# Attention behind a scan: fetching keys a group earlier, dividing the last query pair in SBUF, summing experts in one PSUM bank

## The chip, the cores and the metric

The kernel runs on one core of a Trainium2 chip. A core has a matmul engine (TensorE; PE in the profile, with PEld for its weight loads), a vector engine (DVE), a scalar engine (ACT), GpSimd (POOL) and a sync engine (SP) that here issues nearly all DMAs. Each engine runs its own instructions in order and waits for others by semaphores. SBUF is the working memory, PSUM the memory that TensorE writes. The metric is device time in microseconds (us); lower is better.

## The reference

Input `x` is 4 images of 128 channels and 64 x 64 pixels. Layer 0 is a group norm, a convolution block and a state-space scan (4 groups of channels, 16 states each), added to `x`. Layer 1 takes the 4096 pixels of an image as tokens and does attention with 4 heads and a mixture of 8 experts, of which each token uses 2:

```python
qkv = (x @ W_qkv + b_qkv).reshape(b, n, H, D, 3)
...
scores = jnp.einsum('bhnd,bhmd->bhnm', q, k) * scale
att = jax.nn.softmax(scores, axis=-1)
out = jnp.einsum('bhnm,bhmd->bhnd', att, v)
...
router_probs = jax.nn.softmax(x @ router_w + router_b, axis=-1)
top_p, top_i = jax.lax.top_k(router_probs, K)
...
return jnp.einsum('bnk,bnkc->bnc', top_p, gathered)
```

All is float32.

## The kernel before, in words

**Slots.** Image `b` has 4096 tokens, cut into 8 blocks of 512 (`BLK`, `NB`). One loop of slots (from L1381) runs everything. The scan has 512 units, of two slots each, so `END = 2 * len(units)` is slot 1024; slots behind that have no scan. In a slot the kernel writes out, in a fixed order: sends that have come due (`flush`), the fetch of a scan row (`rows`), a half step of lane X, one group of attention scores, their exponentials, the scan's DVE work, half steps of lane Y, the transposed sums of the scan (`y`), then the value products of the group before (`weighted`) and a second half step of lane X. `queued` (L389) fixes this order on each engine, SP included: what is written first is issued first.

**Attention.** Query blocks go in pairs `q` (1024 queries), key blocks in runs (`RUNS`, L904), since keys become known only as the scan proceeds. A run is cut into parts of one or two key blocks (n = 1 or 2) for each of 4 heads; there are 80 parts an image, 320 in all. A part is worked off in groups of two key tiles (`STEP`, L872), one group a slot: two groups for n = 1, four for n = 2. `load` (L948) fetches a part's queries (`qs`, two buffers; only where head or query pair is new), keys (`ks`, three) and values (`v`, three). L973 decides when the next part is loaded. Where it isn't there when a part begins (keys not yet computed), the part loads for itself and waits two slots.

**The end of a head.** In `weighted` (L1000) the sums of a head and query pair are copied or added from PSUM into `avs`: for each of the two query blocks u, 32 rows of products and 32 rows with the softmax denominator. If more keys are to come, `avs` goes to DRAM as `avd`, to come back as `prev`. Otherwise it goes to DRAM as `total`. When all 4 heads of a pair are there, `inverted` (L1031) loads the denominators packed as `den`, inverts them, stores them as `inverse`, and appends two output tasks, one for each query block.

**Outputs.** `finished` (L1051) is an output task on lane X, or on lane Y behind the scan. It loads `aT` (products), `inv` (inverse denominators, repeated over rows) and `acc` (the residual), multiplies, projects with `wp` into PSUM, adds, normalises, routes, and then applies the experts in four pairs: `share` (a pair's weights, repeated over all partitions by a 512 KB load) times `xf` on DVE, two matmuls with `ew` into the lane's PSUM bank, one DVE add into `res`. Each lane has one PSUM bank.

The last image's last pair (q = 3) runs its keys in one run, (3, 0, 8), behind the scan.

Of the kernel before, what the change touches and what calls it, by code (L numbers as in the profile page):

```python
# [9 lines left out]
F32 = mybir.dt.float32  # L10
# [7 lines left out]
P = 128  # L18
C = 128
EPS = 1e-5  # L20
BLK = 512
NT = BLK // P
# [3 lines left out]
DH = 32  # L26
NH = 4
NE = 8
# [8 lines left out]
def conv_mamba_attn_moe_kernel(ctx: ExitStack, tc: tile.TileContext, t: dict):  # L37
    nc = tc.nc
    x, out = t["x"], t["out"]
    B, _, L = x.shape  # L40
    NB = L // BLK
# [11 lines left out]
    def load(name, shape=None, src=None, eng=nc.sync, pool=const):  # L53
        src = t[name] if src is None else src
        w = pool.tile(list(shape or src.shape), F32, name=f"w_{name}")
        eng.dma_start(out=w, in_=src)
        return w
# [25 lines left out]
    wv, wp, rw, ew, eb8 = (load(k, eng=late) for k in ("wv", "wp", "rw", "ew", "eb8"))  # L83
# [13 lines left out]
    for j in range(4):  # L97
        r = slice(DI * (j % 2), DI * (j % 2) + DI)
# [301 lines left out]
    class Queue:  # L400
# [7 lines left out]
    tensor, vector, scalar, gpsimd, sync = (  # L408
        Queue(e) for e in (nc.tensor, nc.vector, nc.scalar, nc.gpsimd, nc.sync)
    )  # L410

    def mm(out, lhsT, rhs, start=True, stop=True):
        tensor.matmul(out, lhsT=lhsT, rhs=rhs, start=start, stop=stop)
# [8 lines left out]
    def send(out, in_, slots=1):  # L422
        outgoing.append([slots, out, in_])
# [14 lines left out]
    def pool(name, bufs=1, space=None):  # L438
        return main.enter_context(
            tc.tile_pool(name=name, bufs=bufs, **({} if space is None else {"space": space}))  # L440
        )

    att, mix, side = pool("att"), pool("mix"), pool("side")
# [4 lines left out]
    def work(lane, shape=None):  # L448
        return ps_work.tile(shape or [P, BLK], F32, tag=f"work{lane}", name=f"ps_{lane}")

    def tmp(lane, name, shape=None):
        return side.tile(
            shape or [P, BLK], F32, tag=f"tmp{lane}", name=name, bufs=6 if lane == "X" else 4
        )
# [417 lines left out]
    STEP = 2  # L872
# [57 lines left out]
    def attention(b):  # L930

        seen, parts = {}, []
        for q, lo, hi in RUNS:
            known = seen.get(q, 0)
            seen[q] = known + hi - lo
            cuts = [lo, *range(lo + 2 - lo % 2, hi, 2), hi]
            for h in range(NH):  # L940
                for k0, k1 in zip(cuts, cuts[1:]):
                    parts.append((
                        q, h, k0 // 2, k0 % 2, k1 - k0, k0 == lo, k1 == hi, known > 0,
                        seen[q] == NB,
                    ))
        assert all(n == NB for n in seen.values())

        def load(part, qs=None):  # L948
            q, h, k, u, n = part[:5]
            if qs is None:  # L950
                qs = queries(b, q, h)
            return qs, keys(b, h, k, u, n), values(b, h, k, u, n)

        prev = None
        ahead = None
        for at, part in enumerate(parts):
            q, h, k, _, n, first, last, more, final = part
            position[0] = b, parts, at
            if ahead is None:
                while not ready(b, part):  # L960
                    yield None
                ahead = load(part)
                for _ in range(2):
                    yield None
            qs, ks, v = ahead
            ahead = None
            for g in range(0, NT * n, STEP):
                if g == 0 and last:
                    prev = None
                    if more:  # L970
                        prev = att.tile([P, BLK], F32, name="prev", bufs=2)
                        sync.dma_start(out=prev, in_=partial.pop((b, q, h)))
                if g >= NT * n - 3 * STEP and ahead is None and at + 1 < len(parts):  # L973
                    nxt = parts[at + 1]
                    if ready(b, nxt):
                        ahead = load(nxt, qs if nxt[:2] == (q, h) and not nxt[5] else None)
                scs = []
                for j in range(g, g + STEP):
                    sc = ps_sc.tile([P, 2, BLK], F32, name="sc")
                    for u in range(2):  # L980
                        mm(
                            sc[:, u, :], ks[:, j * P : (j + 1) * P],
                            qs[:, u * BLK : (u + 1) * BLK],
                        )
                    scs.append((v[:, j // NT, j % NT, :], sc))
                yield (
                    b, q, h, scs, first and g == 0, last and g + STEP == NT * n, prev, final,
                )

    sums, partial, total, inverse, later = [None], {}, {}, {}, deque()  # L990
# [9 lines left out]
    def weighted(group):  # L1000
        b, q, h, pTs, first, last, prev, final = group
        if first:
            sums[0] = ps_av.tile([P, BLK], F32, name="av")
        av = sums[0]
        for k, (v, pT) in enumerate(pTs):
            for u in range(2):
                mm(
                    av[64 * u : 64 * u + 2 * DH, :], v, pT[:, u, :],
                    first and k == 0, last and k == STEP - 1,
                )  # L1010
        if last:
            avs = att.tile([P, BLK], F32, name="avs", bufs=2)
            if prev is None:
                scalar.copy(avs, av)
            else:
                vector.tensor_add(avs, av, prev)


            if not final:
                partial[b, q, h] = dram.tile([P, BLK], F32, name=f"avd{q}{h}")  # L1020
                send(partial[b, q, h], avs, 3)
                return
            if h == 0:
                total[b, q] = dram.tile([2, 2, NH, DH, BLK], F32, name=f"total{q}")
            d = total[b, q]
            send(d[:, :, h].rearrange("u k r q -> (u k) r q"), avs, 3)
            if h == NH - 1:
                work_left = inverted(b, q)
                later.extend((slot + n, work_left) for n in (4, 6, 8))

    def inverted(b, q):  # L1031

# [15 lines left out]
            ))  # L1048
        yield

    def finished(b, qb, lane):  # L1051

        q, u = divmod(qb, 2)
        td = kqv[b][3]
        s = slice(qb * BLK, (qb + 1) * BLK)
        acc = side.tile([P, NT, C], F32, name="acc", bufs=2)
        aT, inv = tmp(lane, "aT"), tmp(lane, "inv")
        sync.dma_start(out=aT, in_=total[b, q][u, 0].rearrange("h d q -> (h d) q"))
        sync.dma_start(
            out=inv, in_=inverse[b, q][u][:, None, :].to_broadcast([NH, DH, BLK])  # L1060
        )
        sync.dma_start(out=acc.rearrange("p j c -> p (j c)"), in_=td[:, s])
        yield
        yield
        yield
        vector.tensor_mul(aT, aT, inv)
        yield
        ps = work(lane, [P, NT, C])
        for j in range(NT):
            mm(ps[:, j, :], aT[:, j * P : (j + 1) * P], wp)  # L1070
# [4 lines left out]
        ps = transposed(lane, acc)  # L1075
        yield
        xf = tmp(lane, "xf")
        scalar.copy(xf, ps)
        yield
        ps = work(lane, [P, NT, NE])  # L1080
# [45 lines left out]
        ps = work(lane)  # L1126
# [3 lines left out]
        prT = tmp(lane, "prT")[0 : 2 * NE, :]  # L1130
# [16 lines left out]


        ps = work(lane)
        mm(ps, eb8, prT[0:NE, :])  # L1150
        yield
        res = tmp(lane, "res")
        vector.tensor_add(res, ps, xf)
        yield
        ahead = deque(share(e) for e in (0, 2))
        yield
        yield
        for e in range(0, NE, 2):
            if e + 4 < NE:
                ahead.append(share(e + 4))  # L1160
            yield
            w = ahead.popleft()
            if e:
                vector.tensor_add(res, res, ps)
            vector.tensor_mul(w, w, xf[:, None, :].to_broadcast([P, 2, BLK]))
            yield
            ps = work(lane)
            for u in range(2):
                mm(ps, ew[:, e + u, :], w[:, u, :], u == 0, u == 1)
        yield  # L1170
        vector.tensor_add(res, res, ps)
        send(out[b][:, s], res, 2)
        yield

# [94 lines left out]
    lanes, done, running = {"X": deque(), "Y": deque()}, set(), {}  # L1269
# [50 lines left out]
    X, Y = lanes["X"], lanes["Y"]  # L1320
# [9 lines left out]
    for k in range(-2, len(blocks)):  # L1330
        if 0 <= k:
            b, i = blocks[k]
            Y.append((("in", b, i, 1), inputs(b, i, 1), [("scan", *blocks[k - 1], 1)] if k else []))
        if k + 2 < len(blocks):
            b, i = blocks[k + 2]
            if k + 2 == 0 or i > 0:
                upper(k + 2)
        if 0 <= k + 1 < len(blocks):
            b, i = blocks[k + 1]
# [19 lines left out]
    END = 2 * len(units)  # L1359

    rows, due, closing, y_of = {}, deque(), deque(), {}
    h_of, slot = {}, 0
# [18 lines left out]
    while (  # L1381
        slot < END or due or closing or summing or waiting or left or later or lanes["X"] or running
    ):
        at, odd = divmod(slot, 2)
# [10 lines left out]
        if unit and not odd:  # L1395
            h = h_of.pop(at)
# [31 lines left out]
        if waiting:  # L1428
            weighted(waiting)
# [11 lines left out]
    with tc.If(nc.values_load(general[0:1, 0:1]) > 0):  # L1441
# [4 lines left out]
        with tc.For_i(0, B, 1) as b:  # L1446
# [3 lines left out]
                out=t_tok.rearrange("p k c -> p (k c)"),  # L1450
                in_=tsave[bass.ds(b, 1)].rearrange("o p q -> (o p) q"),
            )
            with tc.tile_pool(name="ps_again", bufs=4, space=PSUM) as psum:
                for i in range(NB):
                    ps = anew(t_tok[:, NT * i : NT * (i + 1), :], psum)
# [92 lines left out]
```

## Time and profile before

| what | us |
|---|---|
| median of 3 runs (5158.14 to 5181.4) | 5163.62 |
| the profiled execution's own time | 5160.79 |
| its span, first to last instruction | 5158.6 |
| last DVE instruction of the scan starts at | 4578.8 |
| last attention product ends at | 5087.5 |

The profile is of one execution. It gives each engine's busy time and instruction count, groups of instructions with mean duration and the idle time of the engine before them, and a chain of work followed back from the last instruction. Nearly all instructions were recorded through one helper, so their line reads L406 and they are told apart by the tiles they write and read: `sc<-qs,ks` are scores, `av<-pT,v` value products. A weight load or matmul of 512 columns can stand as two or more records.

| shares of the chain that ended last | |
|---|---|
| PE | 58% |
| DVE | 17% |
| ACT | 11% |
| DMA | 7% |

DMA issues of the tiles that the change touches:

| tile | issues | KB each |
|---|---|---|
| `ks` | 192 and 128 | 512 and 256 |
| `v` | 192 and 128 | 256 and 128 |
| `qs` | 161 | 512 |
| `rows` (the scan's) | 1024 | 512 |
| `share` | 128 | 512 |

### The profile page before, as it was taken

The page shows a single profiled execution, that of the slowest core. Times are in us where ns is not written, and L with a number is a line of the kernel's source. Part 1 is how long each engine was busy: PE and PEld are TensorE (multiplying, and loading weights), DVE is VectorE, ACT ScalarE, POOL GpSimd, SP SyncE. Part 2 cuts the span into 40 slices and gives each one's busy share as a digit, 9 for nine tenths or more (in the row PEclk, how much of TensorE's full clock was granted, in tenths as well). Part 3 has the DMA queues.
Part 4 walks back from the last instruction along what each step waited for, and adds up shares of the span by engine and source line. Part 5 has one row for each costly group of instructions (what it writes and reads, how often), then busy time and mean ns, then how long its engine had stood idle before and what let it go on. Part 6 is the DMA issues. An engine that isn't in the chain of part 4 may idle for free.

```text
span 5158.6 us, 62573 instructions
## 1 busy us (share of the span) xinstructions
PE 4703.0 (91%) x20684; PEld 2317.3 (45%) x20684; DVE 3835.7 (74%) x5780; ACT 3743.0 (73%) x5700; POOL 433.5 (8%) x483
## 2 busy tenths in 40 slices
PE   4567898999999999999999999999999999999997
PEld 2333444444444444444444444444444444443443
DVE  6988767877778878877788787877888887752422
ACT  4556777887787777787878787787788787765453
POOL 1111111110000110010000100010000001000000
PEclk7778999999999999999999999999999999999997
DMA  4556567677666667676766767667866667764532
GB/s 127 182 189 214 206 212 253 234 235 244 232 226 226 232 230 255 230 241 234 265 236 207 235 218 273 239 227 245 286 219 221 221 234 258 239 212 163 177 130 68
DMA packets 451692, 1131.70 MB, mean 219 GB/s; under 512 B 51857, under 2 KB 135330, under 8 KB 451362
## 3 DMA queue, kind: packets, MB, share of 16 engines
q1 hardware_dynamic: 447296, 1125.96, 64.5%
q8 instruction: 166, 2.72, 0.2%
q10 hardware_dynamic: 4066, 1.67, 0.1%
q14 instruction: 164, 1.34, 0.1%
HBM read 967.22 MB, written 143.39 MB: 215 GB/s over the span
## 4 chain that ended last, share of the span: by engine, by line
PE 58%; DVE 17%; ACT 11%; DMA 7%; issue 4%; POOL 2%; SPq 1%; DVEq 0%; ACTq 0%; POOLq 0%
PE av L406 25%; PE sc L406 14%; PE ps_X L406 9%; PE ps_Y L406 6%; PE y L406 6%; DVE h L406 6%; ACT pT L406 4%; ACT L406 3%; DMA ks<-kd 2%; DVE hc L406 2%; DMA rows<-bcd 1%; ACT xt L406 1%; POOL rsX L406 1%; DMA inv<-inverse 1%; DVE stX L406 1%
## 5 line engine op out<-in xcount | busy, mean ns | idle before, releaser
L406 ACT ACTIVATE pT<-sc 128x1024 f32<-128x1024 f32 x2048 | 1984.9, 1023 | 923.4 <-PE sc L406 922.3
L406 PE MATMUL av<-pT,v 128*64 128x512 f32 x8192 | 2003.1, 610 | 6.4 <-DVE avs L406 6.3
L406 PE MATMUL sc<-qs,ks 128*128 128x512 f32 x4096 | 1298.7, 436 | 91.3 <-DMA ks<-kd 47.8
L406 DVE TENSOR_TENSOR_SCAN h<-da,state,h 128x1025 f32<-128x1025 f32 x512 | 1204.2, 2352 | 91.8 <-ACT h L406 58.2
L406 PEld LDWEIGHTS sc<-qs,ks 128*128 128x128 f32 x4096 | 701.1, 190 | 820.2 <-ACT pT L406 272.7
L406 PEld LDWEIGHTS av<-pT,v 128*64 128x64 f32 x8192 | 500.5, 137 | 838.6 <-issue 813.5
L406 ACT ACTIVATE da<-delta,amat 128x512 f32<-128x512 f32 x1024 | 744.4, 731 | 1.9
L406 PE MATMUL y<-ident,hc 128*128 128x128 f32 x4096 | 622.3, 283 | 58.4 <-DVE hc L406 58.4
L406 DVE TENSOR_TENSOR hc<-rows,h 128x1024 f32<-128x1024 f32 x512 | 624.4, 1220 | 15.7 <-PE y L406 5.4
L406 DVE TENSOR_TENSOR h<-rows,du 128x1024 f32<-128x1024 f32 x512 | 623.4, 1218 | 13.0 <-DMA rows<-bcd 13.0
L406 PEld LDWEIGHTS y<-ident,hc 128*128 128x128 f32 x4096 | 520.8, 147 | 219.0 <-issue 76.0
L406 POOL TENSOR_TENSOR rsX<-rsX,mhalf 128x4 f32<-128x4 f32 x92 | 203.7, 2214 | 2668.0 <-DVE rsX L406 2588.7
L406 ACT ACT_TABLE_LOAD x319 | 409.3, 1283 | 19.5 <-DVE zs L406 14.3
L406 POOL TENSOR_TENSOR rsY<-rsY,mhalf 128x4 f32<-128x4 f32 x100 | 132.1, 1321 | 1812.0 <-DVE shiftY L406 1358.4
L406 DVE TENSOR_TENSOR avs<-av,prev 128x512 f32<-128x512 f32 x96 | 66.1, 689 | 224.4 <-PE av L406 201.4
L406 PE MATMUL ps_X<-share,w_ew 128*128 128x512 f32 x432 | 216.0, 623 | 4.1 <-DVE share L406 3.9
L406 ACT ACTIVATE xt<-ps_Y,shiftY,rsY 128x128 f32<-128x128 f32 x380 | 143.9, 471 | 78.4 <-POOL shiftY L406 70.5
L406 DVE TENSOR_TENSOR share<-share,xf 128x1024 f32<-128x1024 f32 x128 | 155.9, 1218 | 23.5 <-DMA share<-sharesX 13.9
L406 DVE SCALAR_TENSOR_TENSOR cm<-y,w_fc1w,cm 128x512 f32<-128x512 f32 x195 | 145.0, 744 | 8.0 <-ACT y L406 4.5
L406 DVE TENSOR_TENSOR res<-res,ps_X 128x512 f32<-128x512 f32 x108 | 73.7, 683 | 99.9 <-PE ps_X L406 99.7
L406 PE MATMUL ps_Y<-pairs,inxc 128*128 128x512 f32 x256 | 131.2, 638 | 15.8 <-DMA pairs<-xn 10.2
L406 ACT COPY state<-h 128x2 f32<-128x2 f32 x448 | 88.9, 198 | 75.5 <-DVE h L406 75.5
(248 smaller groups left out, 3446.4 us busy)
## 6 DMA issues: line engine op xcount, KB each, us to landing
rows<-bcd SPq DMA_DIRECT2D x1024, 512.0 KB
ks<-kd SPq DMA_DIRECT2D x192, 512.0 KB
qs<-qd SPq DMA_DIRECT2D x161, 512.0 KB
share<-sharesX SPq DMA_DIRECT2D x108, 512.0 KB
v<-vd SPq DMA_DIRECT2D x192, 256.0 KB
ks<-kd SPq DMA_DIRECT2D x128, 256.0 KB
avd<-avs SPq DMA_DIRECT2D x96, 256.0 KB
prev<-avd SPq DMA_DIRECT2D x96, 256.0 KB
```

Source lines behind the costliest of these rows:

```text
L406: return lambda *args, **kw: queued(op(*args, **kw))
```

## The change

It has three parts. The next part is loaded when the current one has four groups left, not three. For the last image's last query pair, `weighted` calls a new function `divided`, in place of the way over DRAM: one reciprocal of the whole `avs` tile, two multiplies into two SBUF tiles (in the buffers of the scan's `xin`), and at the last head the two output tasks, which then start with their projection and load only `acc`. An output task that reaches the experts behind the scan (`slot >= END`) lets all eight experts and the bias add up in its PSUM bank, and adds once at the end.

```diff
@@ attention
-                if g >= NT * n - 3 * STEP and ahead is None and at + 1 < len(parts):
+                if g >= NT * n - 4 * STEP and ahead is None and at + 1 < len(parts):
@@ weighted
+            if b == B - 1 and q == NB // 2 - 1:
+                divided(b, q, h, avs)
+                return
             d = total[b, q]
@@ new
+    def divided(b, q, h, avs):
+        if h == 0:
+            quotient.extend(mix.tile([P, BLK], F32, name="xin", bufs=2) for _ in range(2))
+        rec = att.tile([P, BLK], F32, name="prev", bufs=2)
+        vector.reciprocal(rec, avs)
+        for u in range(2):
+            r, d = 64 * u, 64 * u + DH
+            vector.tensor_mul(
+                quotient[u][DH * h : DH * h + DH, :], avs[r : r + DH, :], rec[d : d + DH, :]
+            )
+        if h == NH - 1:
+            for u in range(2):
+                lanes["X"].append((
+                    ("out", b, 2 * q + u),
+                    lambda lane, i=2 * q + u, a=quotient[u]: finished(b, i, lane, a), [],
+                ))
@@ finished
-        aT, inv = tmp(lane, "aT"), tmp(lane, "inv")
...
         sync.dma_start(out=acc.rearrange("p j c -> p (j c)"), in_=td[:, s])
-        yield
-        yield
-        yield
-        vector.tensor_mul(aT, aT, inv)
-        yield
+        if aT is None:
+            aT, inv = tmp(lane, "aT"), tmp(lane, "inv")
...
+            vector.tensor_mul(aT, aT, inv)
+            yield
@@ finished, the experts
-        mm(ps, eb8, prT[0:NE, :])
+        mm(ps, eb8, prT[0:NE, :], True, slot < END)
         yield
-        res = tmp(lane, "res")
-        vector.tensor_add(res, ps, xf)
+        one = slot >= END
+        if not one:
+            res = tmp(lane, "res")
+            vector.tensor_add(res, ps, xf)
...
-            if e:
+            if e and not one:
                 vector.tensor_add(res, res, ps)
...
-            ps = work(lane)
+            if not one:
+                ps = work(lane)
             for u in range(2):
-                mm(ps, ew[:, e + u, :], w[:, u, :], u == 0, u == 1)
+                mm(
+                    ps, ew[:, e + u, :], w[:, u, :], u == 0 and not one,
+                    u == 1 and (not one or e + u == NE - 1),
+                )
         yield
-        vector.tensor_add(res, res, ps)
+        if one:
+            res = tmp(lane, "res")
+            vector.tensor_add(res, ps, xf)
+        else:
+            vector.tensor_add(res, res, ps)
```

## The prediction

> **What bounds the kernel.** I read the page's first two parts, then busy time by stage, then the waits for the tile that the first edit concerns, then the end of the chain.
>
> ```profile
> span 5158.6 us, 62573 instructions
> PE 4703.0 (91%) x20684; PEld 2317.3 (45%) x20684; DVE 3835.7 (74%) x5780; ACT 3743.0 (73%) x5700; POOL 433.5 (8%) x483
> ...
> 650.00:4000.00 3350.00, 3193.20 (x14420) 1577.74 (x14418) 2690.67 (x3946) 2647.05 (x4048) 303.90 (x326) 0.99 0.70 237
> ...
> 4900.00:5087.00 187.00, 186.37 (x735) 76.15 (x733) 37.84 (x93) 103.70 (x112) 2.02 (x2) 1.00 0.31 102
> 5087.00:5159.00 72.00, 34.66 (x88) 17.25 (x84) 29.27 (x83) 3.37 (x7) 2.02 (x2) 0.62 0.29 93
> ```
>
> The last three rows are stretches of the span: length, then busy us of PE, PEld, DVE, ACT, POOL, granted clock, DMA share, GB/s. From 650 us on the matmul engine is the bound: 95% busy to 4000, 99.7% from 4900 to the last attention group at 5087. There an edit is worth only the PE idle time that it removes. Two places have any: waits for keys, and the last 72 us, where every engine is under half busy and latency counts.
>
> **Part 1, the fetch one group earlier.**
>
> ```profile
> L406 PE MATMUL sc<-qs,ks 128*128 128x512 f32 x4096 | 1298.7, 436 | 91.3 <-DMA ks<-kd 47.8
> ...
> 3191.09 0.55 SPq L406 DMA_DIRECT2D qs<-qd  x1
> 3192.71 0.52 SPq L406 DMA_DIRECT2D ks<-kd  x1
> ...
> 3202.64 1.63 PE L406 MATMUL sc<-qs,ks 128*128 128x512 f32 x4 [3.67 <-DMA ks<-kd]
> ```
>
> The group row says that all score matmuls waited 47.8 us for keys: the ceiling of the part. The other three rows are one such wait: the keys are issued at 3192.7, 10 us before PE needs them. Which of these waits does the edit reach? The condition compares g with 4n minus 6 (now 8). A part of one block (n = 1) has g = 0 and 2, and fetches at g = 0 either way; only a part of two blocks (g = 0, 2, 4, 6) moves, from its second group to its first. I paired the 320 key issues with the first score matmul of each of the 320 parts, in order. Behind a two-block part (188): median lead 14.4 us, one wait for keys, 4.3 us (at 461). Behind a one-block part (128): median lead 10.6 us, 35.2 us of waits. Four batch starts: 8.3 us. So the edit reaches 4.3 us directly. Of the 35.2 us, only two waits (4.1 us at 592, 3.3 us at 2904) follow a one-block part whose own load moves up and may clear the queue for them: ceiling 4.3 + 7.4 = 11.7 us, of which 8.4 fall before 650 us, where PE is not the bound. The wait shown is behind a one-block part and stays.
>
> Against it: each moved load is two or three SP issues (qs, ks, v; 1.6 us together) that go ahead of one or two `rows` issues and of sends (`avd`, `bcd`, `tsave`). It can also wait for a buffer: qs has two, so in run (2,6,8), where one two-block part is a whole head, the load now waits for scores of the group just before. Behind that wait stand `rows`, and for `rows` the scan's DVE multiply; but `rows` is fetched three slots of about 4 us (4579 us of scan over 1024 slots) ahead, and SP already stands for DVE's `hc` 1188.5 us in all, so I take nothing. Ends: 8 us gained, 10 lost. I take **1.5 us gained**.
>
> **Part 2, the last division.** Now the end:
>
> ```profile
> 5087.53 0.59 ACT avs L406
> 5088.12 0.02 issue
> 5088.14 5.87 DMA total<-avs
> ...
> 5094.66 2.00 DMA den<-total
> ...
> 5097.07 1.42 DMA inverse<-den
> ...
> 5100.06 8.75 DMA inv<-inverse
> ...
> 5108.91 0.70 DVE aT L406
> 5109.61 0.04 issue
> 5109.65 2.08 PE ps_X L406 x8
> ```
>
> Each row is start, duration, link of the chain. From the end of `av` (5087.51) 22.1 us pass until the second lane's projection starts; 18 are four DMA round trips that go. New on the path: the copy (0.61), a reciprocal 128x512, two multiplies 32x512 (0.69 each, as a 128x512 multiply costs here: time goes by the free size).
>
> The trace has no 128x512 reciprocal. Nearest rows: 128x32 takes 345 ns (median of 16), 128x4 178 ns. Slope 167/28 = 6.0 ns an element, so 0.18 + 508 x 0.0060 = **3.2 us**. The Trainium skill speaks for more: "VectorE: DVE Perf Modes" (First, the fixed hardware budget) has the reciprocal as an iterative divide repeated 8 times; at 0.96 GHz ("Trainium Kernel Development and Optimization", NeuronCore Architecture) an estimate of 512 x 8 / 960 = 4.3 us. I take the rows: at 8.3 ns an element the step from 4 to 32 elements would be 233 ns, not 167.
>
> So lane X's quotient is ready 0.6 + 3.2 + 0.7 = 4.6 us after `av`, lane Y's at 5.3. PE is idle before these matmuls in both kernels and I price them at the slow clock of the rows: 2.08 us, lanes 1.7 apart. X runs from 4.65, Y to 8.4; DVE does X's add and statistics (6.75 to 8.95), then Y's add to 9.64; then transposes, copies, router matmuls as before (5.2 us from projection to router in the chain), so that the second lane's router scores are read at 13.9 us, where the chain now has 5116.95 - 5087.51 = 29.4. Gain **15.5 us** (14.5 by the skill's figure). `acc` needs no time: its load is issued in a queue that is empty from 5053.
>
> What it adds in the loop: heads 0 to 2 each put 4.6 us on DVE, which is 37.8 us busy of the last 187. Heads 1 and 2 have nothing behind them. Head 0 does:
>
> ```profile
> 4923.51 0.59 ACT L406 COPY avs<-av 128x512 f32<-128x512 f32 x1 [0.35 <-PE av L406]
> ...
> 4927.27 1.16 PE L406 MATMUL ps_X<-w_wp,aT 128*128 128x128 f32 x8
> ```
>
> In the new DVE order its reciprocal and two multiplies stand between the `aT` multiplies of the previous pair of outputs (now both at 4918.3). The second then ends at 4924.1 + 3.2 + 1.4 + 0.7 = 4929.5, and the in-order PE, which has the projection at 4927.27, stands there **2.3 us**, with the next scores behind it. By the skill's 4.3 us it would be 3.4. The `total` sends that go were hidden.
>
> **Part 3, one bank.** Four adds of 0.69 us go from each of the 8 outputs behind the scan: 22 us of DVE, no other instruction. For six of them this is worth nothing: 4600 to 4750 has PE at 148.0 of 150 us, and their adds wait for PE, not PE for them (PE waits 1.6 us for `share` from 4600 to 5087). In the last pair it shows:
>
> ```profile
> 5144.19 1.22 DVE L406 TENSOR_TENSOR share<-share,xf 128x1024 f32<-128x1024 f32 x1
> 5145.47 1.98 PE L406 MATMUL ps_Y<-share,w_ew 128*128 128x512 f32 x4
> ```
>
> The multiply ends at 5145.41 and PE starts 0.06 us later: DVE's 0.69 + 1.22 = 1.91 us set the step. Without the add PE sets it, about 1.75 us (pairs of the loop follow at 1.4 to 1.8). Seven steps x 0.16, plus the third multiply no longer waiting for an add: **1.4 us gained**. What is late next is PE, or the fourth `share` loads, which wait for a buffer; ends 0 and 3.
>
> **Sum.** -1.5 - 15.5 + 2.3 - 1.4 = -16.1 us. The profiled execution took 5160.79, so 5144.7. The median of the runs shown, 5163.62, lies 2.8 above it: **5147.5**. 0.5% of it, 26 us, is about what can be told from no change.
>
> **Rivals.**
> - *The moved fetches clear the queue for more* (0.10). All 47.8 us of key waits cannot go, but if half of the 35.2 behind one-block parts did, with the slow-clock stretches that follow the longer ones (about 1.7 us on some 8), the sum is -16 - 18 - 13: 5117. For: nearly all waits are for keys. Against: those loads keep their place and lead.
> - *The end gives back* (0.10): the reciprocal at 4.3 us or more, the PE stall over 3.4 us with a slow clock behind it, part 1 losing 10. -14 + 5 + 10: 5164, no change.
> - *Slower* (0.09): bunching. Where one-block and two-block parts alternate, loads now follow at 2 and 4 slots, not 3 and 3, and hold SP for qs and v buffers. If the parts behind two blocks then waited as those behind one block do (39.2 us of idle before 128 of them, 0.31 us each, against 17.2 before 188), 188 x 0.31 - 17 = 40 us, with some 20 us of slow clock: 5160.8 - 16 + 60, about 5208 by the median. It decides from 42 us on. Against: their load only gains lead.
> - *The edit does not do what it says*: for part 1 that is my forecast, since 128 of 320 fetches, with three quarters of the waits, don't move.
>
> My forecast has 0.71, its own range 5135 to 5158, with 0.05 below 5138. So: faster by over 0.5% 0.10 + 0.05 = 0.15; within, 0.66 and the second rival's 0.10, 0.76; slower 0.09. The range for 8 in 10 takes in the forecast's ends and the second rival: 5132 to 5164.
>
> **What would show it.** Last `av` to the end: 71 us now, about 54 expected. A DVE reciprocal 128x512 of 3.2 us. A PE wait of 2 to 3 us for `aT` at head 0 of the last query pair. Key waits behind one-block parts still near 35 us. I am wrong if they fall under 20, if waits for `rows` grow past 13 us by tens, or if the end shrinks by under 12.

## The result, and the profile after

| | before | changed |
|---|---|---|
| median of 8 runs, us | 5163.22 | 5148.12 |
| lowest to highest, us | 5158.14 to 5181.4 | 5139.97 to 5153.02 |
| profiled execution, us | 5160.79 | 5142.79 |
| its span, us | 5158.6 | 5140.9 |

The ratio is 0.997, 95% interval [0.996, 0.9979]: 15 us faster by the medians, 11 to 21 by the interval. That is a real gain, and inside the 0.5% that was called no change.

The profile's first lines and the score group, then two stretches of the span (length, busy us of PE, PEld, DVE, ACT, POOL, granted clock, DMA share, GB/s):

```profile
span 5140.9 us, 62489 instructions
PE 4700.3 (91%) x20684; PEld 2317.8 (45%) x20684; DVE 3827.3 (74%) x5749; ACT 3741.0 (73%) x5700; POOL 432.9 (8%) x483
...
L406 PE MATMUL sc<-qs,ks 128*128 128x512 f32 x4096 | 1296.4, 435 | 85.5 <-ACT pT L406 42.9
...
4900.00:5090.00 190.00, 187.03 (x736) 76.34 (x734) 40.29 (x86) 104.26 (x113) 2.01 (x2) 1.00 0.30 100
5090.00:5141.00 51.00, 30.12 (x88) 15.25 (x84) 26.77 (x75) 3.36 (x7) 2.01 (x2) 0.70 0.28 95
```

PE does the same work in the same number of instructions. The last product now ends at 5090.5, and 50.5 us follow it where 71.1 followed. The stretch before it holds 3 us of PE idle time where it held 0.6: the price paid in the loop.

The end, in the chain of work (start, duration, link):

```profile
5090.51 0.59 ACT avs L406
...
5091.13 3.36 DVE prev L406
...
5094.52 0.70 DVE xin L406
...
5095.26 2.09 PE ps_X L406 x8
```

`prev` is the buffer of the reciprocal. Copy, reciprocal, one multiply: 4.8 us from the last product to the first projection, with no DMA. Three stretches in the columns above show what I had not priced:

```profile
5095.00:5100.00 5.00, 4.64 (x20) 4.24 (x20) 3.45 (x13) 0.07 (x1) 0.40 (x1) 0.50 0.01 3
5100.00:5103.00 3.00, 2.41 (x20) 2.29 (x20) 2.34 (x16) 1.31 (x3) 1.61 (x2) 0.98 0.01 3
5103.00:5111.00 8.00, 1.26 (x6) 0.60 (x7) 6.50 (x37) 0.83 (x3) 0.00 (x0) 0.53 0.01 2
```

PE is busy for 5 us in a row at half clock, is then granted the full clock for about 3 us, and does the router matmuls in it. The second lane's router scores are read 12.2 us after the last product (29.5 before). In the profile of before the router matmuls ran at half clock:

```profile
5113.00:5117.00 4.00, 3.84 (x19) 3.72 (x18) 1.62 (x12) 1.02 (x3) 1.01 (x1) 0.50 0.00 0
```

That is not a mark of the old code, though. Three of the kernels below have the old end up to the router (lead only, bank only, lead shortened), and in each of their profiles the clock is full for 3.4 us, from 26.4 to 26.7 us after the last product on. They read these scores at 28.0, 28.4 and 28.3 us. Against them the change saves 16.0 us up to the router.

And the place in the loop (the timeline, in brackets the idle time before and what ended it):

```profile
4924.69 3.35 DVE L406 RECIPROCAL prev<-avs 128x512 f32<-128x512 f32 x1 [5.14 <-ACT avs L406]
...
4928.07 1.38 DVE L406 TENSOR_TENSOR xin<-avs,prev 32x512 f32<-32x512 f32 x2
4929.48 0.69 DVE L406 TENSOR_TENSOR aT<-aT,inv 128x512 f32<-128x512 f32 x1
...
4930.23 1.16 PE L406 MATMUL ps_X<-w_wp,aT 128*128 128x128 f32 x8 [2.33 <-DVE aT L406]
```

Four DVE instructions in their written order (the row of `xin` holds two), and the matmul that waits 2.33 us for the last of them.

### The profile page after: what moved, and what is told of

Same layout as the page of the kernel before. It is cut to its first block, busy times and chain, and to the rows that moved or that the text cites. A ratio compares the mean times of both kernels' runs of the same rounds, so it can differ in the third digit from the quotient of the medians.

```text
span 5140.9 us, 62489 instructions
## 1 busy us (share of the span) xinstructions
PE 4700.3 (91%) x20684; PEld 2317.8 (45%) x20684; DVE 3827.3 (74%) x5749; ACT 3741.0 (73%) x5700; POOL 432.9 (8%) x483
## 2 busy tenths in 40 slices
DMA packets 450332, 1129.57 MB, mean 220 GB/s; under 512 B 51521, under 2 KB 134994, under 8 KB 450002
## 4 chain that ended last, share of the span: by engine, by line
PE 61%; DVE 16%; ACT 10%; DMA 6%; issue 4%; POOL 2%; SPq 1%; DVEq 0%; ACTq 0%; POOLq 0%
PE av L406 25%; PE sc L406 14%; PE ps_X L406 9%; PE ps_Y L406 6%; PE y L406 6%; DVE h L406 5%; ACT pT L406 3%; DMA ks<-kd 3%; ACT L406 3%; DVE hc L406 2%; ACT xt L406 1%; POOL rsX L406 1%; DVE du L406 1%; DVE stX L406 1%; DMA inv<-inverse 1%
## 5 line engine op out<-in xcount | busy, mean ns | idle before, releaser
L406 DVE TENSOR_TENSOR avs<-av,prev 128x512 f32<-128x512 f32 x96 | 66.2, 689 | 238.7 <-PE av L406 218.7
L406 PE MATMUL ps_Y<-pairs,inxc 128*128 128x512 f32 x256 | 133.6, 648 | 14.4 <-DMA pairs<-xn 8.7
L406 PEld LDWEIGHTS ps_X<-share,w_ew 128*128 128x128 f32 x432 | 73.9, 190 | 143.9 <-issue 94.0
```

The costliest lines, as they stand in the source:

```text
L406: return lambda *args, **kw: queued(op(*args, **kw))
```

## The experiments

A warning first, which shaped them. Kernels whose loop up to slot 1024 is the same code differ by as much as the change is worth: in the division-only and bank-only kernels below, score matmul 3584 of 4096 (at 4602.7 us in the profile of before) came 14.7 and 11.5 us later than in the kernel before. So the medians of many runs, with their intervals, judge the loop; single profiles judge only a wait or the end. Each ratio is to the kernel before, run beside it on the same chip; it is not exactly the quotient of the two medians.

**One part alone.** Three kernels, each the one before with one part of the change; the diffs are hunks of the change shown above:

```diff
# lead only
-                if g >= NT * n - 3 * STEP and ahead is None and at + 1 < len(parts):
+                if g >= NT * n - 4 * STEP and ahead is None and at + 1 < len(parts):
# division only: `divided`, and its call in `weighted` and `finished`
# bank only: `one = slot >= END` and what hangs on it
```

> The kernel before with the fetch at four groups left, nothing else changed. Theory (the moved fetches reach almost no wait): 0 to 4 us faster than before; key waits ahead of score matmuls 40 to 48 us in all, those behind one-block parts still 30 to 36 us; last attention product to the end 71 us as before. Rival (the earlier fetch clears the queue, and the 9 us by which the changed kernel's attention ran ahead between 620 and 4850 us come from it): 8 to 12 us faster, and the same drift of the score matmuls against the kernel before. Rival (bunching): slower, waits for rows above 13 us by tens.

> The kernel before with the last pair divided in SBUF, nothing else. Theory: last product to the end falls from 71 to about 53 us (22 us of DRAM trips against 4.7 us, and a router stage partly at the full clock), a PE wait for aT of 2.3 us at head 0 of the last pair: 15 us faster. Rival (the end of the loop and the experts share the gain, so the division alone brings less than 12): 8 to 12 us faster.

> The kernel before with experts summed in one bank behind the scan, nothing else. Theory: the steps of the last pair fall from 1.9-2.0 us to 1.72 us, last product to the end from 71 to about 68.5 us; nothing in the loop, where PE is 99% busy: 2 to 3 us faster. Rival (22 us of DVE gone from 8 outputs shorten the loop too): 6 us or more, with less PE idle time between 4600 and 4900 us.

| kernel | median, us | ratio, interval | last product to end, us |
|---|---|---|---|
| before | 5163.52 (54 runs) | 1 | 71.2 (its profile) |
| lead only | 5158.93 | 0.9991 [0.9984, 0.9998] | 66.2 |
| division only | 5155.41 | 0.9979 [0.9968, 0.999] | 51.5 |
| bank only | 5164.47 | 1.0001 [0.9991, 1.0012] | 64.7 |

The division carries the gain: 11 us, interval 5 to 17. That is nearer to the 8 to 12 of its rival than to the 15 expected, and the interval doesn't part the two. The lead-only kernel is 1 to 8 us faster, 5 by the medians: more than none, but not clearly the 8 to 12 of its rival, and no bunching (waits for `rows` were 14.9 us against 13.0). That it is the lead which brings these 5 us is not shown, as the shortened lead below will show. The waits for keys behind it stayed, 38 us behind one-block parts. The bank's 2 to 3 us can't be told from nothing in the medians; its rival, 6 us or more, is out.

The last column corrects a reading of my own. The lead-only kernel has the end of the kernel before unchanged, and took 66.2 us there, not 71.2. Two things in the end are not the same each time. A landing of `share` in the chain took 7.7 us in the profile of before and 4.0 us in that of the lead-only kernel. And the clock stayed at half from 3.2 to 54.4 us after the last product in the one, where in the other it came back for 3.4 us at 26.4 and again at 46.9. One profile of the end is not a measure. By three profiles with that end (71.2, 66.2, and 66.0 below) it takes 67.8 us on average, and in two of the changed kernel (50.5, 51.2) 50.8 (50.3, 50.7 and 52.5 in three more kernels with its end): the end is worth 17 us, not the 21 of the two profiles side by side.

**Lead shortened.** The kernel before with two groups left, the lead of a one-block part:

```diff
-                if g >= NT * n - 3 * STEP and ahead is None and at + 1 < len(parts):
+                if g >= NT * n - 2 * STEP and ahead is None and at + 1 < len(parts):
```

> The kernel before with the fetch of a two-block part's successor at two groups left, the lead that one-block parts have. Theory (waits for keys come of a lead of two slots, about 10 us, against a landing of about the same): waits behind two-block parts rise from 4.3 us to 30 to 60 us, with slow-clock stretches behind the longer ones; 25 to 80 us slower. Rival (the waits come of what else is queued around one-block parts, a new qs, prev, avd, and not of the lead): waits behind two-block parts stay under 15 us, under 10 us slower.

It was not slower: 5160.6 us, 0.9992 [0.9984, 1.0]. My theory fell, and its rival held. A lead shortened by one group comes out like a lead lengthened by one (0.9991), so these runs put neither difference down to the lead. The waits of the scores for keys in its trace (engine, what it waited for: us in total, times, longest):

```profile
PE sc L406 <- DMA ks<-kd: 55.0, 22, 6.0
```

By parts: 8.9 us behind two-block parts (4.3 before), 37.2 behind one-block parts, 8.9 at batch starts. A lead of two slots alone makes hardly a wait. What one-block parts have besides is a crowd: the wait shown in the prediction, at 3202.6, has these stretches in the kernel before (columns as above):

```profile
3185.00:3190.00 5.00, 5.00 (x28) 3.01 (x27) 4.81 (x6) 3.70 (x7) 1.99 (x2) 1.00 1.07 376
3190.00:3195.00 5.00, 4.67 (x23) 2.32 (x22) 3.10 (x4) 4.95 (x8) 0.00 (x0) 1.00 1.05 363
3195.00:3200.00 5.00, 3.90 (x22) 1.81 (x19) 2.93 (x3) 3.87 (x6) 0.00 (x0) 1.00 0.99 349
```

The last column but one is the busy share of the DMA engines: full for 15 us, over 340 GB/s. Each one-block part there brings its own queries (512 KB) and `prev` (256 KB) beside keys and values. In the 8 us behind the issue of the keys, the DMA engines were busy 1.0 of the time (median) for the 14 loads behind one-block parts that PE waited for, 0.89 for the 114 others. But the lead in time differs as well: from the issue of the keys until PE stood ready for them, 6.5 us (median, at most 8.4) for the 14, 10.8 for the 114. Short lead and full queue come together at these waits. How much each does was not parted; a lead of two slots without the crowd was not enough.

**The lead undone, and the division moved.** The changed kernel again, the same with the lead at three groups, and with the division of heads 0 to 2 written two slots later:

```diff
-                divided(b, q, h, avs)
+                if h < NH - 1:
+                    later.append((slot + 2, divided(b, q, h, avs)))
+                else:
+                    for _ in divided(b, q, h, avs):
+                        pass
                 return
```

> The changed kernel itself, beside the others of this call: 14 to 16 us under the kernel before, as measured already; last product to the end 50 to 52 us.

> The changed kernel with the fetch put back to three groups. Theory (the fetch is worth at most a few us, the division about 12, the bank 2): 0 to 5 us slower than the changed kernel, and 9 to 14 us faster than before. Rival (the fetch alone carries half of the gain): 7 us or more slower than the changed kernel.

> The changed kernel with the division of heads 0 to 2 written two slots later, head 3 at once. Theory (the reciprocal at head 0 stands ahead of the second aT multiply on DVE and costs PE 2.3 us): the PE wait for aT at the last pair but one goes, the score matmuls behind it come 2.4 us earlier, 2 to 3 us faster than the changed kernel. Rival (the division collides with other DVE work later, or the wait is taken over by another): no gain, a new PE wait of 1 us or more in the following 12 us.

| kernel | median, us | ratio, interval |
|---|---|---|
| before | 5161.95 | 1 |
| changed, again | 5149.07 | 0.9974 [0.9967, 0.9982] |
| lead at three groups | 5150.54 | 0.9977 [0.9971, 0.9984] |
| division two slots later | 5142.07 | 0.9958 [0.9944, 0.9971] |

From this side the lead is worth 1.5 us, with intervals that overlap: it can't be told from nothing. With the late division the wait is gone, as the rows of its timeline show:

```profile
4926.87 0.69 DVE L406 TENSOR_TENSOR acc<-ps_Y,acc 128x512 f32<-128x512 f32 x1 [5.92 <-PE ps_Y L406]
...
4928.63 1.16 PE L406 MATMUL ps_X<-w_wp,aT 128*128 128x128 f32 x8
```

Against the changed kernel's first profile its score matmuls go from 0.8 us behind to 1.6 ahead over this place: 2.4 us. The medians say 7, over the 2 to 3 expected; what is over 2.4 I can't place, and the intervals of the two kernels overlap.

**A lead for all parts.** If a short lead is part of it, four groups of lead for one-block parts as well should end the waits. SBUF had no room for more two-block buffers, so keys and values went into buffers of one block (5 and 6), the third query buffer was paid for with them and with one of lane X's six temporaries:

```diff
-                if g >= NT * n - 4 * STEP and ahead is None and at + 1 < len(parts):
-                    nxt = parts[at + 1]
-                    if ready(b, nxt):
-                        ahead = load(nxt, qs if nxt[:2] == (q, h) and not nxt[5] else None)
+                new = at + 1 + len(ahead)
+                covered = NT * n - g + sum(NT * p[4] for p in parts[at + 1 : new])
+                if covered <= 4 * STEP and new < len(parts):
+                    fetch_next(new)
```

> The changed kernel with loads kept four groups ahead also where parts have one block: keys and values in buffers of one block each (5 and 6), three query buffers, one buffer fewer for lane X's temporaries. Theory (waits behind one-block parts come of a DMA queue that is full for 8 to 10 us there, and of a lead of two slots against it): waits for keys behind one-block parts fall from 33 us to under 12, half-clock stretches between 650 and 5080 us from 82 to under 60; 15 to 40 us faster than the changed kernel. Rival (the transfers are as many and collide elsewhere, twice as many key transfers of half the size): waits for keys stay over 20 us or move to rows, within 10 us of the changed kernel.

> The changed kernel with the buffers of the deeper fetch (keys and values by one block, three query buffers, one buffer fewer for lane X), but its own rule of when to fetch. Theory (the lead does it, not the buffers): waits for keys stay at 28 to 38 us behind one-block parts, within 5 us of the changed kernel. Rival (the third query buffer or the smaller transfers do it): waits for keys under 20 us in all, 10 us or more faster than the changed kernel.

> Loads kept four groups ahead for all parts, and the division of heads 0 to 2 two slots later: the two edits together. Theory (they act at different places): 26 us (the loads) plus 2.4 us faster than before, 5131 to 5135 us, so 14 to 18 us under the changed kernel. Rival (the loads' gain was partly the spread of the runs): 5137 to 5142 us.

| kernel | median, us | before, beside it | ratio, interval | key waits behind one-block parts, us |
|---|---|---|---|---|
| changed (first profile) | 5148.12 | 5163.22 | 0.997 [0.996, 0.9979] | 32.9 |
| one-block buffers, old rule | 5161.41 | 5165.69 | 0.9995 [0.9986, 1.0003] | 29.6 |
| lead for all parts | 5135.26 | 5161.95 | 0.9947 [0.9933, 0.9961] | 3.3 |
| lead for all, late division | 5132.84 | 5165.69 | 0.9945 [0.9931, 0.9958] | 3.7 |

The waits of PE with the lead for all parts:

```profile
PE sc L406 <- DMA ks<-kd: 11.1, 5, 3.4
```

The five that are left all belong to parts that load for themselves, at the start of an image or where keys were not yet computed; this lead can't reach those. Against the kernel that has the same buffers, waits for keys fell by 27 us and the time by 26 (5161.4 to 5135.3, on two chips; ratio 0.9995 to 0.9947). The two numbers are close by chance, as the profiles of the two kernels show, one-block buffers first:

```profile
span 5159.0 us, 63000 instructions
PE 4711.0 (91%) x20684; PEld 2324.7 (45%) x20684; DVE 3826.9 (74%) x5749; ACT 3743.4 (73%) x5700; POOL 436.4 (8%) x483
```

```profile
span 5131.1 us, 62999 instructions
PE 4700.1 (92%) x20684; PEld 2314.8 (45%) x20684; DVE 3824.8 (75%) x5749; ACT 3742.3 (73%) x5700; POOL 439.1 (9%) x483
```

Of the 28 us between the spans, 11 are PE busy time in the same number of instructions, with less time at half clock (116.1 and 88.7 us between 650 and 5080). The other 17 are PE idle time: 27 of keys less, and 10 of other waits more.

The buffers themselves cost 11 us against the changed kernel's ratio (0.9995 and 0.9974), more than the 5 that I had allowed. So the lead for all parts is 14 us under the changed kernel run beside it (5149.07), a little less than the 15 to 40 expected. My further expectation, half-clock stretches under 60 us, was wrong: 88.7 us, in the changed kernel's profiles 81.9 and 102.4. The last kernel is the best of the study, 5132.84 us, 28 us under the kernel before by its ratio; what the late division adds to it can't be told.

**What the buffers cost.** The changed kernel with five temporaries for lane X and nothing else; and the best kernel with all six back, paid for with one of the three `share` buffers:

```diff
# one
-            shape or [P, BLK], F32, tag=f"tmp{lane}", name=name, bufs=6 if lane == "X" else 4
+            shape or [P, BLK], F32, tag=f"tmp{lane}", name=name, bufs=5 if lane == "X" else 4
# the other
-                w = side.tile([P, 2, BLK], F32, name="share", bufs=3)
+                w = side.tile([P, 2, BLK], F32, name="share", bufs=2)
```

> The changed kernel with five, not six, temporaries for lane X, nothing else. Theory (the 12 us that the kernel with block-sized buffers lost come of its 128 to 192 more key and value transfers of half the size): within 4 us of the changed kernel. Rival (the missing buffer holds lane X up and with it the queues): 8 us or more slower than the changed kernel.

> The kernel with deeper loads and the late division, lane X with all six temporaries again, paid for by two buffers for the expert shares instead of three. If the missing temporary cost 8 us or more: under 5128 us. If not: 5130 to 5140 us, the third share buffer being what the end of an output waits for.

Five temporaries: 5154.92 us, ratio 0.9974 [0.9963, 0.9985], that of the changed kernel. The temporary cost nothing that shows, with an interval of 6 us to either side; what is left for the 11 us are the smaller key and value transfers (481056 DMA packets in every kernel with one-block buffers, 450332 in the changed one) and the third query buffer, which I did not part.

Two `share` buffers: 5178.12 us, 1.002 [1.001, 1.003], 45 us over the best kernel by the medians (39 by the ratios, on two chips) and over both ranges that I gave. SP's waits, of the best kernel and then of this one:

```profile
SPq L406 <- PE ps_X L406: 81.8, 46, 7.6
```

```profile
SPq L406 <- PE ps_X L406: 209.2, 69, 11.5
...
SPq L406 <- DVE share L406: 120.5, 38, 7.7
```

SP stands for the matmuls and multiplies that read the two buffers (for the multiplies 40.2 us in the best kernel), and behind it stands everything else that SP issues: PE's waits for `pairs`, the input of the scan's projections, rise from 11.2 to 32.7 us. Key waits did not rise (12.2 us after 12.7): it is another transfer that is late. PE's waits for `share` rise by 9, and PE is busy 11 us longer, with half-clock stretches of 105.8 us after 81.9. These three make up the 42 us between the two profiles.

## Why the prediction was right

5147.5 us was forecast and 5148.12 measured; the steps:

- **Where time can be had.** Right: PE busy time is the same to 3 us, and what moved for certain is PE idle time in the end and at head 0.
- **Part 1, 1.5 us.** The sum can't be told from nothing: 5 us [1, 8] from one side, 1.5 from the other, and a shorter lead came out like the longer one. The waits behind one-block parts stayed (32.9 us; 31.3 in the second profile of the changed kernel), as the code said. But the three waits that the edit was to reach stayed too: 4.3, 4.1 and 3.3 us before, 3.4, 3.7 and 2.9 in the changed kernel. So "reaches 4.3 us directly" was wrong, and that the small sum fits is luck. I had sorted the waits by the size of the part before them, and not by whether a load was ahead at all. The first two waits are of parts that load for themselves, as the issues of their keys in the profile of before show:

```profile
453.98 0.51 SPq L406 DMA_DIRECT2D ks<-kd  x1
...
585.57 0.51 SPq L406 DMA_DIRECT2D ks<-kd  x1
```

  The last scores of the parts before them had ended at 358 and 540 us; the keys that they load had gone to DRAM (`kd`) only at 444 and 576 us, so that no longer lead reaches these two. My reason for the other waits, a short lead, left out the full DMA queue that stands beside it. That SP's added waits cost nothing held here: `rows` waits were 11.0 us, 13.4 in the second profile. The kernel with two `share` buffers shows what they cost where they are long.
- **Part 2, the reciprocal.** 3.2 us from the slope of two short rows; 3.35 measured. The 8 repeats of the Trainium skill ("VectorE: DVE Perf Modes", First, the fixed hardware budget), an estimate of 4.3 us, were too much here.
- **Part 2, the end, 15.5 us.** The mechanism held, and so did the size. Router scores were read at 12.2 us, not 13.9. The term was PE's clock, taken as slow throughout: in the 3 us at full clock the second lane's transposes took 0.66 us and its router matmuls 1.04, in the profile of before 1.12 and 1.85. But the old end was priced from a profile that had no such stretch, while the three others have it, so the term drops out of the difference but for half a microsecond: 16.0 us saved.
- **Part 2, the wait of 2.3 us.** 2.33 measured; moved away by the late division.
- **Part 3, 1.4 us.** The size can't be told. From the start of the second `share` multiply to the end of the last add it is 14.4 to 16.7 us in the ten profiles with the bank (mean 15.5) and 15.7 to 17.5 in the four without (mean 16.5): 1.0 us by the means, with ranges that overlap. What is shown is the step without its add. The steps became 1.72 us, as this stretch of the chain of the changed kernel shows:

```profile
5126.84 1.72 PE ps_Y L406 x4
5128.55 1.72 PE ps_X L406 x4
5130.27 1.72 PE ps_Y L406 x4
```

- **The first rival**, more from a clear queue, was right that these waits can be had, but through an edit that this change does not make: the lead for all parts took 29 of the 33 us. It also priced them too high, 31 us for half of the waits and their slow clock; that edit brought 26 us, on equal buffers, for nearly all.

The forecast is 16 us of gain, the measured one 15 with an interval of 11 to 21. That the two medians are 0.6 us apart is luck within that interval. Its large term, the end, rests on a mechanism that the runs show; part 1 had none.

## What to carry to other kernels

An edit to a prefetch is worth what it does to the transfers that are waited for: pair each wait with the code path that issued its load before counting on it, and set aside the loads whose data is not there any earlier. Here three quarters of the waits were on a path that the edit left alone, and an edit to that path removed them. Work put on an engine for a later gain goes into that engine's order: look at what stands behind it there, and at who waits for that. And when SBUF is short, ask of each buffer who stands for it: here a third buffer for `share`, for which the issuing queue stands, was worth some 40 us, and a sixth temporary nothing that shows.

## What was not expected of the hardware

- The matmul clock can come back within the end of a kernel: in the changed kernel after 6.8 us at half, of which 5 dense, 3.4 us at full, then half again for 20.5 us. What brings it back stays open. By the profile of before PE was busy throughout the 3.4 us from 23.7 us after the last product on, and the clock stayed at half; in that of the lead-only kernel it was busy throughout the 3.4 us from 23.0 on, and 3.4 us at full followed.
- A DVE reciprocal of 128x512 float32 takes 3.35 us, 4.9 times a multiply of that size (0.69): 6.3 ns an element between 32 and 512, as between 4 and 32.
- The loop is not the same length twice: the last product ends at 5090.5 us in the first profile of the changed kernel and at 5096.7 in its second, the same code; with five temporaries, whose ratio is the same (0.9974), at 5105.6. Differences of up to 15 us between the loops of two single profiles say nothing.
